# A merged attention and expert kernel, planned with other costs for TensorE's products

## The chip, the cores and the metric

The kernel runs on one core of one Trainium2 chip. The metric is the device time of one execution in microseconds (us). A core has five engines that each take their instructions strictly in the order written: TensorE (PE in the profile, its weight loads as PEld), VectorE (DVE), ScalarE (ACT), GpSimd (POOL) and SyncE (SP, which here only issues DMAs). [...]the order in which the program hands instructions to each engine decides a good part of the time.

## What is computed

The input is x of 8 sequences x 512 tokens x 128 features, float32. Four residual layers follow each other:

```
x = x + attention_a(layernorm(x))   # 16 heads of 8: convolution of 4 taps, silu, delta rule over time
x = x + experts(layernorm(x))       # "f": 8 experts of 256, the best 2 of each token
x = x + attention_b(layernorm(x))   # linear attention in chunks of 128, features elu+1, 16 heads
x = x + experts(layernorm(x))       # "g": the same weights as "f"
```

The delta rule is a recurrence over the 512 tokens of a sequence. For each head with an 8x8 state S:

```
v_new = (v_t - k_t S) * b_t
S     = S + outer(k_t, v_new)
o_t   = q_t S
```

An expert layer computes logits, takes each token's two best experts, and sums relu(x W1[e]) W2[e] with the two normalised weights.

## The kernel before

**Tiling.** Time is cut into 8 chunks (c = 0 to 7) of 64 tokens; a chunk holds 8 sequences x 64 tokens = 512 rows, that is 4 blocks of 128. All 128 pairs of sequence and head lie on the 128 partitions for the recurrence. Each chunk passes through these streams of work:

- `prepare(c)` (L712): layer norm, the convolution as 4 products per q, k, v (`s_pp_a`, L811), silu, norms and the reordering through DRAM.
- `recurring()` (L970): the delta rule, 4 tokens at a time, 16 steps per chunk, 128 in all. A step is four VectorE instructions that depend on each other: `pj`, `factors`, `terms`, `st` (L1003 to L1022). The outputs of a chunk are products on GpSimd (`po`, L1050), summed on VectorE (`o`, L1069).
- `ending(c)` (L1080), then for the chunk `layers` (L1692): output projection (`s_po_a`), experts f (`moe`, L1228), attention b (`linear_attention`, L1661, and `attend`, L1536), experts g. Four lanes hold four chunks at once.
- `moe` sorts the token rows by expert with indirect DMAs on GpSimd, loads the weights of 15 blocks of 128 rows, and does per block two products 128 wide into `s_ph` (L1448), relu on ScalarE into `hT`, and two products into `y_py` (L1460). For the second expert layer of chunk 6, and both expert layers of chunk 7 (which goes in two halves), all experts are computed densely (`all_experts`, L1128), with products 512 or 256 wide.
- `attend` has per block two products `s_pc_b` 512 wide (L1578), whose reader is VectorE's `qs_b`, a `s_pp_b` 384 wide, and products 144 wide (`s_pu_b`, `s_pS_b`).

**What sets the order.** Nothing is ordered by the hardware or by a compiler. While the program is written out, class `Weaver` (L97) plays all streams against each other on an imagined clock per engine. Every instruction goes through `Timed` (L333), which is why nearly all rows of the profile say L343, and `Timed` asks `duration` (L357) what the instruction takes: a pair of time on the engine and of a lag until a reader on another engine may begin. `Weaver.run` (L180) always continues a stream that can begin within `ahead` of the earliest; among those it takes the one with the largest sum of "chain behind it" and a value that `FAVOURED` gives for its part (for instance `("recur", 3)`, the recurrence of chunk 3). The emitted order is then each engine's instruction order.

`tile_hybrid_block_kernel` (L387) first plans without emitting: `PLANS` = 4 rounds, in which the chain behind a step is the longest path of durations from it to the end (`behind`, L216). Then come `PASSES`: 1 round and 35 rounds more in which the chain behind is replaced by the time before the end at which the step begins when the plan is played backwards with busy engines (`before_end`, L224). A last round with `FAVOURED` and `AHEAD_OF` emits the program.

**Filling products.** Before each TensorE instruction, `Weaver.run` hands the planned gap on TensorE to `keep_busy` (L1724). If the gap is at least 0.6 us and a PSUM bank is free, it emits products of a bf16 matrix of ones with itself, 512 wide, whose result nobody reads (`busy`, L1735). Their number follows from the planned gap, and 0.22 us is planned for each:

```
n = int(BUSY * gap / 0.22)        # L1730, BUSY = 0.7
```

**The cost of a TensorE product** in `duration` is, before:

```
if op == "transpose":
    return key, 0.2, 0.15
return key, max(free_size(args[2]) * 1.75e-3, 0.27), 0.15
```

`args[2]` is the moving operand, so `free_size` is the product's width: 128, 144, 256, 384 or 512. A product in the program is one call of `pe.matmul` and is charged once.

Of the kernel before, what the change touches and what calls it, by code (L numbers as in the profile page):

```python
# [19 lines left out]
P = 128  # L20
# [19 lines left out]
PREPARED_ON_POOL = ()  # L40
VALUES_ON_POOL = ()
ADDED_ON_PE = ()
AHEAD_OF = 0
PLANS = 4

LANDS = 3.4
ROWS_LAND = 3.8

PASSES = (
    (1, 0.0, {}),  # L50
    (35, 0.1, {}),
)

FAVOURED = {
    ("b", 0): 365, ("b", 3): 20, ("b", 4): 25, ("b", 5): -8, ("b", 6): -10, ("b", 7): -22, ("b", 7.5): 10,
    ("beside",): -5,
    ("ending",): 4,
    ("f", 0): -43, ("f", 1): 17, ("f", 2): -3, ("f", 3): -3, ("f", 4): -3, ("f", 5): 15, ("f", 6): 309, ("f",
    7): -32, ("f", 7.5): 29,
    ("g", 0): -5, ("g", 3): -13, ("g", 4): -37, ("g", 5): -2, ("g", 6): -15, ("g", 7): 321, ("g", 7.5): 170,  # L60
    ("prepare", 0): -5, ("prepare", 1): -2, ("prepare", 2): -22, ("prepare", 3): 10, ("prepare", 5): -6,
    ("prepare", 7): -10,
    ("recur", 0): 105, ("recur", 1): 98, ("recur", 2): -19, ("recur", 3): -7, ("recur", 4): 10, ("recur", 5):
    -47, ("recur", 6): 15, ("recur", 7): -28,
    ("values",): 14,
}

HALVED = (7,)
# [264 lines left out]
class Timed:  # L333
# [5 lines left out]
    def __getattr__(self, op):  # L339
        call = getattr(self.engine, op)  # L340

        def issue(*args, **kw):
            r = call(*args, **kw)  # L343
            self.weaver.took(*duration(self.key, op, args, kw))
            return r

        return issue


def free_size(ap):  # L350
    n = 1
    for d in ap.shape[1:]:
        n *= d
    return n


def duration(key, op, args, kw):  # L357
    if op == "dma_start":
        return key, 0.4, 0.0, None, LANDS
    if op == "value_load":  # L360
        return key, 0.75, 0.0
    if op == "indirect_dma_start":
        return key, 1.3, 0.0, None, ROWS_LAND
    if key == "PE":
        if op == "transpose":
            return key, 0.2, 0.15
        return key, max(free_size(args[2]) * 1.75e-3, 0.27), 0.15
    out = args[0] if args else kw["out"]
    n = free_size(out)
    if op == "tensor_reduce":  # L370
        n = free_size(args[1])
    if key == "ACT":
        table = TABLE_OF.get(args[2]) if op == "activation" else None
        return key, (0.39 if "bias" in kw else 0.2) + n * 0.76e-3, 0.1, table
    if key == "POOL" and ALU.pow in args:
        return key, 1.05, 0.1
    if key == "POOL":
        return key, 0.15 + n * (1.8e-3 if n > 512 else 2.2e-3), 0.1
    if op == "reciprocal":
        return key, 0.15 + n * 6.5e-3, 0.0  # L380
    if op == "bn_stats":
        return key, 0.28, 0.0
    return key, 0.16 + n * 1.04e-3, 0.0
# [3 lines left out]
def kernel(ctx: ExitStack, tc: tile.TileContext, *tensors: bass.AP):  # L387
# [9 lines left out]
    for n, ahead, favoured in PASSES:  # L397
        for _ in range(n):
# [3 lines left out]
            chains.update(weaver.before_end())  # L402
    merged(ctx, tc, Weaver(chains, FAVOURED, AHEAD_OF), *tensors)

# [1389 lines left out]
```

## Time and profile before

| what | value |
|---|---|
| median of three runs | 951.38 us (951.37 to 951.84) |
| the profiled execution's own time | 1007.78 us |
| its span, first to last instruction | 1006.1 us |
| mean granted TensorE clock | 0.919 |
| instructions | 14877, of these TensorE products 4144 |
| busy: PE, PEld | 834.4 us (83%), 540.9 us (54%) |
| busy: DVE, ACT, POOL | 655.4 us (65%), 523.7 us (52%), 476.3 us (47%) |
| last recurrence step begins (`terms`) | 788.2 us |

The profiled execution takes 1007.78 us where the plain runs take 951.38 us, so a time from the profile stands to a plain one about as 1 to 0.944. The span is 1.7 us shorter than the execution's time.

How to read the rows: a group of instructions names engine, operation and "out<-in" by the program's tiles, then shapes, "x" with their number, busy time and the mean ns of one, then how long the engine had been idle before them and what ended it. Products on PE are pipelined: two in a row overlap, so the sum of busy time is not the sum of their durations, and the distance at which they can follow each other is read from the start times in the timeline. A table by stage gives for each stretch the busy time of each engine with its instruction count, the granted TensorE clock as a fraction of full, the busy share of the DMA engines and GB/s.

### The profile page before, as it was taken

To read this page: it belongs to the slowest core of one execution; us is meant where nothing else is said; L and a number is where in the kernel's file an instruction comes from. 1 tells how busy PE (TensorE), PEld (TensorE's weight loads), DVE (VectorE), ACT (ScalarE), POOL (GpSimd) and SP (SyncE) were. 2 spreads that over 40 slices of the span, in tenths; PEclk is the share of its full clock that TensorE was granted. 3 is DMA by queue.
4 is the path that set the end of the run, shared out by engine and by line. 5 is a ranking of instruction groups with operands and counts; after the bars stand their busy time and mean duration, and the time that the engine had idled before them with its cause. 6 is when DMAs were issued, how large, how long until landed. Compare 5 with 4: busy or idle time off the path is not lost.

```text
span 1006.1 us, 14877 instructions
## 1 busy us (share of the span) xinstructions
PE 834.4 (83%) x4144; PEld 540.9 (54%) x4144; DVE 655.4 (65%) x1625; ACT 523.7 (52%) x1464; POOL 476.3 (47%) x615
## 2 busy tenths in 40 slices
PE   8978697688898887888787788779876848999998
PEld 3332242537453676447643575547745737776566
DVE  1377878648898487788788796688774812264520
ACT  4343255665656456765385475753752526435343
POOL 1133136254646434774367635774366442554530
PEclk9989799799899789899988898989998969999999
DMA  1404504586206464367615574763635636611111
GB/s 27 101 21 116 159 6 127 159 228 189 57 4 178 126 204 129 96 174 222 164 53 161 161 223 126 197 190 102 202 113 155 201 107 169 170 54 48 37 48 38
DMA packets 157989, 126.83 MB, mean 126 GB/s; under 512 B 53105, under 2 KB 123730, under 8 KB 157906
## 3 DMA queue, kind: packets, MB, share of 16 engines
q1 hardware_dynamic: 150674, 112.16, 39.6%
q0 software_dynamic: 6656, 13.64, 4.7%
q8 instruction: 33, 0.54, 0.2%
q14 instruction: 50, 0.41, 0.1%
q10 hardware_dynamic: 576, 0.08, 0.0%
HBM read 91.70 MB, written 36.23 MB: 127 GB/s over the span
## 4 chain that ended last, share of the span: by engine, by line
PE 37%; DVE 28%; ACT 11%; issue 7%; DMA 5%; POOL 5%; another core or an unknown queue 4%; SPq 2%; ACTq 0%; DVEq 0%; POOLq 0%
PE s_ph_g L343 5%; PE y_py_g L343 5%; PE y_py_f L343 4%; PE s_pc_b L343 4%; PE s_pu_b L343 3%; PE s_ph_f L343 3%; DVE st L343 3%; ACT squares L343 3%; DVE factors L343 3%; PE s_pp_a L343 2%; POOL po L343 2%; DVE terms L343 2%; SPq L343 2%; DVE pj L343 2%
## 5 line engine op out<-in xcount | busy, mean ns | idle before, releaser
L1735 PE MATMUL busy<-ones 128*128 128x512 bf16 x514 | 131.5, 403 | 5.3 <-DVE sbd L343 2.4
L343 POOL TENSOR_TENSOR po<-st,kq 128x256 f32<-128x256 f32 x128 | 94.8, 768 | 5.7 <-DVE o L343 5.5
L343 PE MATMUL s_pp_a<-xnT_a,wc 128*128 128x512 f32 x192 | 92.6, 621 | 0.6 <-ACT xnT_a L343 0.6
L343 POOL COPY st<-st 128x64 f32<-128x64 f32 x31 | 8.0, 257 | 175.9 <-DVE st L343 165.5
L1735 PEld LDWEIGHTS <-ones 128*128 128x128 bf16 x514 | 52.1, 104 | 71.3 <-issue 27.2
L343 POOL TENSOR_TENSOR kv_b<-ph_b,v 128x1024 f32<-128x1024 f32 x32 | 63.1, 1974 | 56.8 <-DVE ph_b L343 31.7
L343 PE MATMUL y_py_f<-wt_f,hT_f 128*128 128x128 f32 x420 | 64.7, 308 | 21.5 <-ACT hT_f L343 19.7
L343 ACT ACTIVATE hT_g<-s_ph_g 128x512 f32<-128x512 f32 (+1 forms) x96 | 48.5, 511 | 62.8 <-PE s_ph_g L343 38.2
L343 DVE TENSOR_REDUCE st<-terms 128x64 f32<-128x320 f32 x128 | 62.1, 485 | 24.8 <-ACT terms L343 7.9
L343 ACT COPY terms<-st 128x64 f32<-128x64 f32 x128 | 39.5, 309 | 74.5 <-DVE st L343 64.8
L343 PE MATMUL s_pc_b<-kv_b,tri 128*128 128x512 f32 x128 | 69.7, 648 | 10.3 <-POOL kv_b L343 6.7
L343 PEld LDWEIGHTS y_py_f<-wt_f,hT_f 128*128 128x128 f32 x420 | 58.6, 218 | 28.0 <-ACT hT_f L343 23.6
L343 POOL DMA_INDIRECT there<-m_xw_f,rows_f x56 | 55.9, 999 | 34.2 <-ACT m_xw_f L343 17.6
L343 ACT ACTIVATE hT_f<-s_ph_f 128x512 f32<-128x512 f32 (+1 forms) x88 | 43.7, 501 | 52.8 <-PE s_ph_f L343 38.7
L343 POOL DMA_INDIRECT m_g_f<-back,rows_f x56 | 56.1, 1002 | 31.3 <-issue 15.1
L343 PE MATMUL y_py_g<-wt_g,hT_g 128*128 128x128 f32 x360 | 50.3, 288 | 20.9 <-issue 11.1
L343 DVE TENSOR_REDUCE o<-po 128x64 f32<-128x512 f32 x64 | 42.9, 679 | 34.5 <-POOL po L343 34.5
L343 PE MATMUL s_ph_f<-xsT_f,wt_f 128*128 128x128 f32 x420 | 60.7, 298 | 5.5 <-ACT xsT_f L343 4.5
L343 DVE TENSOR_REDUCE factors<-pj 128x32 f32<-128x288 f32 x128 | 58.8, 460 | 7.4 <-ACT factors L343 3.8
L343 PEld LDWEIGHTS s_ph_f<-xsT_f,wt_f 128*128 128x128 f32 x420 | 56.5, 211 | 10.5 <-ACT xsT_f L343 6.3
L343 PEld LDWEIGHTS s_pp_a<-xnT_a,wc 128*128 128x128 f32 x192 | 36.2, 198 | 43.8 <-issue 37.7
L343 PE MATMUL s_ph_g<-xsT_g,wt_g 128*128 128x128 f32 x360 | 52.2, 296 | 9.0 <-ACT xsT_g L343 3.4
(312 smaller groups left out, 1989.3 us busy)
## 6 DMA issues: line engine op xcount, KB each, us to landing
wt_f<-w SPq DMA_DIRECT2D x105, 256.0 KB
wt_g<-w SPq DMA_DIRECT2D x90, 256.0 KB
scr<-y_a SPq DMA_DIRECT2D x24, 256.0 KB
m_xs_f<-there SPq DMA_DIRECT2D x21, 256.0 KB
back<-yb_f SPq DMA_DIRECT2D x21, 256.0 KB
m_xs_g<-there SPq DMA_DIRECT2D x18, 256.0 KB
back<-yb_g SPq DMA_DIRECT2D x18, 256.0 KB
qk<-scr SPq DMA_DIRECT2D x16, 256.0 KB
```

Source lines behind the costliest of these rows:

```text
L343: r = call(*args, **kw)
L1735: nc.tensor.matmul(pt, ones, ones.unsqueeze(1).to_broadcast([P, 4, P]), start=True, stop=True)
```

## The change

Four settings of the planner change, and nothing else. The streams, tiles, DMAs and arithmetic are the same; the order on each engine and the number of filling products follow anew from the plan.

- A TensorE instruction is planned at 0.9e-3 us per column of its moving operand, at least 0.05 us, widths between 128 and 256 counted as 256, a transpose as 128 wide. Its lag until a reader begins is 0.3 us instead of 0.15 us.
- `PASSES` is empty, so the chains are those of the four rounds of longest paths.
- `AHEAD_OF` is 0.05 us instead of 0.
- `FAVOURED` has other values.

```diff
-AHEAD_OF = 0
+AHEAD_OF = 0.05
...
 PASSES = (
-    (1, 0.0, {}),
-    (35, 0.1, {}),
 )
 
 FAVOURED = {
-    ("b", 0): 365, ("b", 3): 20, ("b", 4): 25, ("b", 5): -8, ("b", 6): -10, ("b", 7): -22, ("b", 7.5): 10,
-    ("beside",): -5,
-    ("ending",): 4,
...
-    ("recur", 0): 105, ("recur", 1): 98, ("recur", 2): -19, ("recur", 3): -7, ("recur", 4): 10, ("recur", 5):
-    -47, ("recur", 6): 15, ("recur", 7): -28,
-    ("values",): 14,
+    ("b", 0): 8, ("b", 1): -301, ("b", 2): -68, ("b", 3): -134, ("b", 4): -200, ("b", 5): -81, ("b", 6): -92,
+    ("b", 7): -216, ("b", 7.5): 390,
+    ("beside",): 215,
+    ("ending",): -74,
...
+    ("outputs",): 217,
...
+    ("recur", 0): -852, ("recur", 1): -89, ("recur", 2): 37, ("recur", 3): -27, ("recur", 4): -282, ("recur",
+    5): -197, ("recur", 6): -116, ("recur", 7): 291,
+    ("values",): 12,
 }
...
     if key == "PE":
-        if op == "transpose":
-            return key, 0.2, 0.15
-        return key, max(free_size(args[2]) * 1.75e-3, 0.27), 0.15
+
+        n = P if op == "transpose" else free_size(args[2])
+        n = 2 * P if P < n < 2 * P else n
+        return key, max(n * 0.9e-3, 0.05), 0.3
```

More of the change, by code (lines that the diff above doesn't have):

```diff
@@ L49 @@
 PASSES = (
-    (1, 0.0, {}),
-    (35, 0.1, {}),
 )
 FAVOURED = {
-    ("b", 0): 365, ("b", 3): 20, ("b", 4): 25, ("b", 5): -8, ("b", 6): -10, ("b", 7): -22, ("b", 7.5): 10,
-    ("beside",): -5,
-    ("ending",): 4,
[L58 to L62, printed above, removed]
-    ("recur", 0): 105, ("recur", 1): 98, ("recur", 2): -19, ("recur", 3): -7, ("recur", 4): 10, ("recur", 5):
-    -47, ("recur", 6): 15, ("recur", 7): -28,
-    ("values",): 14,
+    ("b", 0): 8, ("b", 1): -301, ("b", 2): -68, ("b", 3): -134, ("b", 4): -200, ("b", 5): -81, ("b", 6): -92,
+    ("b", 7): -216, ("b", 7.5): 390,
+    ("beside",): 215,
+    ("ending",): -74,
+    ("f", 0): 2, ("f", 1): 5, ("f", 2): -46, ("f", 3): 79, ("f", 4): 25, ("f", 5): -77, ("f", 6): 105, ("f",
+    7): 30, ("f", 7.5): 245,
+    ("g", 0): 97, ("g", 1): 75, ("g", 2): -94, ("g", 3): 110, ("g", 4): -172, ("g", 5): -398, ("g", 6): -132,
+    ("g", 7): 190, ("g", 7.5): 15,
+    ("outputs",): 217,
+    ("prepare", 0): -61, ("prepare", 1): 150, ("prepare", 2): 32, ("prepare", 3): 24, ("prepare", 4): -223,
+    ("prepare", 5): -10, ("prepare", 6): 38, ("prepare", 7): -418,
+    ("recur", 0): -852, ("recur", 1): -89, ("recur", 2): 37, ("recur", 3): -27, ("recur", 4): -282, ("recur",
+    5): -197, ("recur", 6): -116, ("recur", 7): 291,
+    ("values",): 12,
 }
```

## The prediction

> **What bounds the kernel now.** I read the page's chain first. It belongs to no single engine:
>
> ```profile
> PE 37%; DVE 28%; ACT 11%; issue 7%; DMA 5%; POOL 5%; another core or an unknown queue 4%; SPq 2%; ACTq 0%; DVEq 0%; POOLq 0%
> ```
>
> Then the table by stage, cut where the recurrence ends (790 us) and where TensorE fills up (850 us), and the same table for the filling products alone:
>
> ```profile
> 0.00:200.00 200.00, 158.65 (x624) 72.41 (x624) 127.36 (x309) 88.03 (x258) 55.35 (x132) 0.91 0.33 89
> 200.00:790.00 590.00, 487.09 (x2575) 332.37 (x2575) 454.32 (x1089) 339.81 (x944) 329.49 (x379) 0.91 0.54 152
> 790.00:850.00 60.00, 39.14 (x251) 33.44 (x250) 20.91 (x70) 27.68 (x72) 26.45 (x31) 0.80 0.51 145
> 850.00:1006.00 156.00, 149.56 (x700) 102.64 (x698) 52.77 (x158) 68.22 (x193) 65.00 (x75) 1.00 0.24 67
> ```
>
> ```profile
> 0.00:200.00 200.00, 91.38 (x367) 0.91 0.33 89
> 200.00:790.00 590.00, 35.45 (x132) 0.91 0.54 152
> 790.00:850.00 60.00, 4.09 (x13) 0.80 0.51 145
> 850.00:1006.00 156.00, 0.59 (x2) 1.00 0.24 67
> ```
>
> Columns of the first, after the length: PE, PEld, DVE, ACT, POOL busy, then granted clock. In the middle PE is busy 83% and VectorE 77%: two engines near full that wait for each other. From 850 us on PE is busy 96% at full clock, while VectorE has 53 us to do in 156: that stage ends when PE ends. Fillers are dense only at the start. From 200 us on there are 147 of the 514, so the old plan saw hardly a gap on PE there.
>
> **What a product costs on the chip.** The groups by shape and the timeline of the last stage:
>
> ```profile
> L343 PE MATMUL s_pc_b<-kv_b,tri 128*128 128x512 f32 x128 | 69.7, 648 | 10.3 <-POOL kv_b L343 6.7 <-DVE shift_g L343 3.0 <-DVE ph_b L343 0.2
> ```
>
> ```profile
> 453.01 1.11 PE L343 MATMUL y_py_f<-wt_f,hT_f 128*128 128x128 f32 x8
> 454.06 0.51 PE L343 MATMUL s_pu_b<-v,ph_b 64*128 64x144 f32 x2
> 454.50 0.51 PE L343 MATMUL s_pu_b<-sbd,ident 128*128 128x144 f32 x2
> ```
>
> ```profile
> 934.13 1.02 PE L343 MATMUL s_ph_g<-wt_xsT_g,wc 128*128 128x512 f32 x2
> 934.99 1.02 PE L343 MATMUL s_pc_b<-kv_b,tri 128*128 128x512 f32 x2
> 935.85 1.02 PE L343 MATMUL y_py_g<-hT_g,wc 128*128 128x512 f32 x2
> 936.71 0.81 PE L343 MATMUL s_pp_b<-wb,xn_xnT_b 128*128 128x384 f32 x2
> ```
>
> The program has 8 chunks x 4 blocks x 2 = 64 products `s_pc_b`; the trace has 128. So each float32 product is two instructions on PE. Starts of 512-wide products lie 0.86 us apart (934.99 to 935.85): 0.43 per instruction, 0.86 per product. Four products 128 wide take 1.05 us (453.01 to 454.06), so about 0.25 each; one 144 wide takes 0.44. (Transposes are one instruction, 0.11 apart in the rows of the same timeline.) Against that:
>
> - 512 wide: 0.86 on the chip, planned 0.896 before, 0.461 after.
> - 128 wide: 0.25, planned 0.27 before, 0.115 after.
> - 144 wide: 0.44, planned 0.27 before, 0.23 after.
> - transpose: 0.11, planned 0.2 before, 0.115 after.
>
> The new cost is the distance between two instructions in a row, charged once per product: right for transposes, half the truth for the products.
>
> Here a rule speaks for the change. The Trainium skill, Perfetto Trace Analysis, section Engine Utilization, gives the array 307.2 G output elements a second, halved for FP32_LOW_HIGH. Read as the price of a whole product, 128x512 elements at 153.6 G/s are 0.43 us, and the new 0.461 is right. Then the fillers below would find real gaps and the sum would be no more than the clock's gain. The rows say 0.43 per instruction with two instructions per product, and I follow the rows.
>
> **The change, part by part.** *Planned PE time.* From the instruction counts by shape, two per float32 product: 231 products 512 wide, 138 of 256, 33 of 384, 876 of 128, 188 of 144, 97 narrower than 10, 439 transposes, 65 small bf16 ones. Before, in that order: 207 + 62 + 22 + 237 + 51 + 26 + 88 + 18 = 711 us planned. After: 106 + 32 + 11 + 101 + 43 + 5 + 51 + 3 = 352 us. On the chip at full clock, with 0.1 per narrow instruction and 0.06 per bf16 one: 199 + 59 + 21 + 219 + 83 + 19 + 48 + 4 = 652 us. The old plan is 9% above the chip, the new one 46% below.
>
> *Filling products.* Their number is worked out from planned gaps. I take 951 us for the old plan's length, an estimate: gaps 951 - 711 = 240 us, of which 514 x 0.22 = 113 us, or 47%, were filled. After, a plan of the same length has 951 - 352 = 599 us of gaps; the same share is 281 us, some 1,280 fillers. If the plan shrinks to 800 us, gaps are 448, filled 210 us, 955 fillers. So 440 to 765 are added; I take 600. On the chip 26 of them start over 5.7 us at full clock (31.87 to 37.59 in the timeline), 0.22 each, so 132 us are added to an engine already busy 83% of the span. Shared out like PE's busy time without fillers (67, 452, 35 and 149 us by stage): 13, 85, 7 and 28 us.
>
> *What hides them.* PE is idle 41, 103, 21 and 6 us in the four stages. But a filler stands in PE's queue ahead of a real product, and the plan's gaps aren't the chip's, since real products take twice as long as planned. I let half of the idle time absorb fillers where it is long: 20, 51, 10, and all 6 in the last.
>
> *The clock.* With more fillers PE stays warm. The clock is granted at 0.91 in the first two stages, 0.80 in the third: bringing all to 1.00 would save 14, 44 and 8 us of PE's busy time. The Trainium skill, TensorE: Matmul & The Clock Gate, section HAM oscillation, says that idle gaps beyond about 3.4 us throttle the array; by it, full warmth is worth those 66 us on PE. The row limits it: the last stage already has 1.00 with 2 fillers, so it gains nothing, and PE is 37% of the chain. I take two thirds of it, 9, 29 and 5 us.
>
> First stage 13 - 20 - 9, at best nothing to pay; second 85 - 51 - 29 = 5; third 7 - 10 - 5, nothing; last 28 - 6 = 22. I count no gain from the surplus, since no chain of PE's alone runs through it. Together **+27 us**. Bounds: 440 fillers with all idle time absorbing give no loss and the clock's gain, 25 us (37% of 66); 765 fillers with a quarter absorbed cost about 85.
>
> *Readers.* VectorE reads each 512-wide `s_pc_b`. A pair takes 1.02 us from start to end; planned until the reader begins are 0.461 + 0.3 = 0.761 after (1.046 before). The reader `qs_b` is put into VectorE's queue 0.26 us early, and behind it in order stand the recurrence's four instructions, `o`, and the routing's small ones: 64 x 0.26 = **+17 us** on an engine busy 77%. Rows of 8 products, 2 us on the chip and 0.9 planned, do the same to ScalarE's `hT`, which has 48% free; nothing there, with 20 us if `terms` is what stands behind. Bounds of readers: 0 (covered by idle time) to 35.
>
> *Order by `FAVOURED`, no `PASSES`, `AHEAD_OF`.* No instruction is added, but all move, in every queue: SP's weight loads and row stores, GpSimd's indirect DMAs and `po`, ScalarE's table switches. No row prices that. The nearest bounds: VectorE is idle 136 us in the middle, and the recurrence needs 1.79 us (418 + 460 + 423 + 485 ns) x 128 = 229 us of the 738 it spans, so a better order could end it earlier by tens of us; a worse one costs as much. One further wait like VectorE's `o` on `po` (20 us in the middle) is the nearest size. I take 0, ends -25 and +25.
>
> Sum: 1007.78 + 27 + 17 = 1052 us for a profiled execution; times 951.38 / 1007.78 = 0.944: **993 us**.
>
> **The rivals.** A, the sum, 0.62. B: fillers sink into idle time, the order is somewhat worse, with one more wait of 20 us: 1028 x 0.944 = 970 us, 0.17. For it: PE idles 171 us. Against: its idle in the last stage is 6. C, the other side: warmth. If the fillers fit and hold the clock at 1.00, 25 us come off the chain; with an order that ends the recurrence some 20 us earlier, 963 x 0.944 = 909; clock alone 928. It decides if added fillers cost less than 66 us of PE plus the idle time they fall in, chiefly if few go into the last stage. For it: the plan still knows VectorE's times, and PE's cheapness puts VectorE's chain first. Against: all the products' ends are planned too early. 928 us, 0.16. D, the plan comes out nearly alike: 951 us, 0.05; against it, half of PE's planned time is gone.
>
> **How the numbers follow.** Measurement tells apart about 0.2%, 2 us. Faster 0.16, same 0.05, slower 0.79. Range 935 to 1045: the low end takes in B and C's half nearer to no change; the high end is 1007.78 + 85 + 35 less 20 for idle time that both would use, 1108, times 0.944. Outside lie half of C, 0.08, and the worse end of A with a worse order, about 0.1.
>
> **What would show it.** Fillers between 950 and 1,300, most after 200 us; clock above 0.96; PE busy over 90% in the middle; PE's last stage longer than 156 us or with dozens of fillers. Wrong if fillers stay near 514 (the sum's main term falls), if the clock rises and PE's busy time doesn't, or if the last recurrence step begins well before 788 us.

## The result, and the profile after

The changed kernel takes 1008.95 us (median of three runs, 1005.69 to 1010.35) where the kernel before takes 951.38. The ratio is 1.060, with a 95% interval of 1.056 to 1.064: 58 us slower. Forecast were 993 us and slower.

The first profile of before, on which the prediction was built, turned out to be of an execution of 1007.78 us, 6% longer than its timed runs. A second profile of the same kernel has an execution of 953.93 us, and it is the one to hold against the profile after (1005.69 us). The chain of waits of the changed kernel, and below it that of the second profile of before:

```profile
PE 63%; DVE 20%; issue 6%; ACT 5%; POOL 4%; DMA 1%; SPq 0%; DVEq 0%; ACTq 0%; POOLq 0%
```

```profile
PE 34%; DVE 32%; ACT 11%; POOL 7%; issue 6%; DMA 6%; SPq 2%; DVEq 0%; ACTq 0%; POOLq 0%
```

TensorE's share of the chain nearly doubled, VectorE's fell from 32% to 20%. The stages now (a stage is a stretch of the execution), cut at 200 us and where the last recurrence step ends (columns as in the prediction's first table: length, PE, PEld, DVE, ACT, POOL busy, granted clock, DMA share, GB/s), first the changed kernel, then the second profile of before:

```profile
0.00:200.00 200.00, 172.18 (x699) 82.69 (x700) 117.10 (x280) 88.42 (x247) 52.93 (x127) 0.91 0.35 94
200.00:774.00 574.00, 529.31 (x2869) 340.41 (x2868) 426.53 (x1049) 325.90 (x900) 314.07 (x369) 0.95 0.53 150
774.00:1004.00 230.00, 220.99 (x1165) 156.25 (x1164) 102.96 (x298) 113.95 (x317) 109.02 (x119) 1.00 0.33 96
```

```profile
0.00:200.00 200.00, 159.84 (x634) 74.22 (x635) 128.58 (x311) 89.75 (x262) 57.21 (x134) 0.91 0.34 91
200.00:750.00 550.00, 475.48 (x2564) 325.45 (x2563) 453.29 (x1088) 339.13 (x938) 327.75 (x376) 0.93 0.56 162
750.00:952.20 202.20, 184.93 (x950) 132.55 (x948) 73.86 (x228) 95.69 (x265) 92.87 (x106) 0.99 0.34 96
```

The middle is 24 us longer and the stage after the recurrence 28 us. In the middle PE is busy 92% instead of 86%, VectorE 74% instead of 82%. The fillers went from 514 to 1,099; their group in the profile after, and what of it lies in the last stage (the changed kernel, then the second profile of before):

```profile
L1737 PE MATMUL busy<-ones 128*128 128x512 bf16 x1099 | 268.8, 392 | 6.6 <-DVE ph_b L344 3.2
```

```profile
774.00:1004.00 230.00, 17.27 (x68) 1.00 0.33 96
```

```profile
750.00:952.20 202.20, 4.21 (x15) 0.99 0.34 96
```

The last stage is longer because the new order leaves more for it: without fillers 1,097 TensorE instructions instead of 935, and 298 of VectorE instead of 228, with TensorE busy 96% of it.

The largest waits of VectorE for a TensorE product, in total us, number and longest wait; the changed kernel first, then the second profile of before:

```profile
DVE sbd L344 <- PE s_pu_b L344: 34.8, 26, 5.3
DVE qs_b L344 <- PE s_pc_b L344: 27.1, 31, 3.4
DVE x_a L344 <- PE s_po_b L344: 19.5, 7, 7.0
DVE dn_b L344 <- PE s_pS_b L344: 18.3, 13, 3.6
DVE x_a L344 <- PE s_pty_g L344: 14.8, 2, 10.0
DVE up_f L344 <- PE y_pl_f L344: 10.6, 5, 7.3
```

```profile
DVE x_a L343 <- PE s_pty_g L343: 37.6, 3, 17.2
DVE qs_b L343 <- PE s_pc_b L343: 20.8, 20, 6.8
DVE sbd L343 <- PE s_pu_b L343: 17.0, 21, 2.9
DVE dn_b L343 <- PE s_pS_b L343: 10.3, 8, 3.9
DVE x_a L343 <- PE s_po_a L343: 10.0, 5, 7.1
DVE qs_b L343 <- PE s_pk_b L343: 9.4, 6, 3.2
DVE x_a L343 <- PE s_po_b L343: 3.0, 3, 1.8
```

Not every one of these waits grew. Summed over all such rows, stage by stage:

| VectorE waits for TensorE, us | before, second profile | changed kernel |
|---|---|---|
| to 200 us | 4.1 | 10.1 |
| the middle | 29.7 | 60.4 |
| after the recurrence | 81.6 | 63.8 |
| the whole span | 115.5 | 134.2 |

The middle is where they count. There VectorE's busy time fell by 27 us (453.3 to 426.5) and its waits for all engines rose by 51 (69.9 to 121.2), of which 31 for TensorE; the difference is the 24 us by which the middle grew.

The longest of the 26 waits at `sbd` (their mean is 1.3 us), seen from both queues of the changed kernel. VectorE first, then TensorE over the same stretch (start, us, instruction, number):

```profile
647.99 0.30 DVE L344 TENSOR_TENSOR sbd<-s_pu_b,hmask 128x144 f32<-128x144 f32 x1
648.20 0.41 DVE L344 TENSOR_TENSOR ph_b<-s_pp_b,mn_b 128x256 f32<-128x256 f32 x1
653.93 0.31 DVE L344 TENSOR_TENSOR sbd<-s_pu_b,hmask 128x144 f32<-128x144 f32 x1 [5.32 <-PE s_pu_b L344]
...
656.66 0.41 DVE L344 TENSOR_TENSOR pj<-st,factors 128x256 f32<-128x256 f32 x1
```

```profile
644.64 2.77 PE L344 MATMUL s_ph_g<-xsT_g,wt_g 128*128 128x128 f32 x12
647.20 2.87 PE L344 MATMUL y_py_g<-wt_g,hT_g 128*128 128x128 f32 x16
650.00 1.03 PE L344 MATMUL s_pn_a<-sq,hmask 128*16 128x512 f32 x2
650.96 2.05 PE L344 MATMUL s_ph_g<-xsT_g,wt_g 128*128 128x128 f32 x16
652.95 0.51 PE L344 MATMUL s_pu_b<-v,ph_b 64*128 64x144 f32 x2
```

The table by stage over two parts of that stretch (the clock is the third number from the end):

```profile
644.00:649.00 5.00, 5.00 (x25) 5.00 (x25) 4.41 (x10) 3.06 (x7) 3.29 (x5) 0.50 0.17 46
650.00:653.00 3.00, 3.00 (x20) 2.03 (x19) 0.00 (x0) 1.35 (x3) 3.00 (x4) 1.00 0.74 186
```

VectorE stands still for 5.32 us at `sbd`, and the next recurrence step, `pj`, starts only at 656.66 behind it. TensorE is not idle and runs no filler: it works off 6 + 8 + 1 + 8 real products ahead of `s_pu_b`. The new cost plans these at 0.69 + 0.92 + 0.46 + 0.92 = 3.0 us; from 644.64 to 652.95 they took 8.3. At full clock, by the distances that the prediction read off, they would take about 6.4 (an estimate: 22 x 0.25 + 0.86); the rest goes with the granted clock of 0.50 up to 649 us. So the price is not all of this wait, but the larger part of the 5.3 us that were lost against the plan.

The planner's own clock can be laid beside the trace, since VectorE's 1,611 planned instructions stand in the trace in the order in which they were emitted, alike in kind one by one. Before this `sbd` it has VectorE idle for 0.40 us. Before all 56 `sbd` that read `s_pu_b` it plans 4.4 us of idle time, where the chip waits 34.8 (kernel before: 5.6 planned, 17.0 on the chip); before `qs_b` 4.9, where the chip waits 30.9 for `s_pc_b` and `s_pk_b` (before: 28.7 planned, 30.2 on the chip). At `qs_b` the old plan foresaw the waits, the new one did not.

### The profile page after: what moved, and what is told of

Its sections match the earlier page's. It is cut to its first block, busy times and chain, and to the rows that moved or that the text cites. A ratio compares the mean times of both kernels' runs of the same rounds, so it can differ in the third digit from the quotient of the medians.

```text
span 1004.0 us, 16075 instructions
## 1 busy us (share of the span) xinstructions
PE 922.5 (92%) x4729; PEld 579.4 (58%) x4729; DVE 646.6 (64%) x1625; ACT 528.3 (53%) x1463; POOL 476.0 (47%) x615
## 4 chain that ended last, share of the span: by engine, by line
PE 63%; DVE 20%; issue 6%; ACT 5%; POOL 4%; DMA 1%; SPq 0%; DVEq 0%; ACTq 0%; POOLq 0%
PE s_pp_a L344 8%; PE busy L1737 7%; PE s_ph_g L344 7%; PE y_py_g L344 6%; PE s_ph_f L344 6%; PE y_py_f L344 6%; PE s_pc_b L344 5%; PE s_pu_b L344 4%; DVE spare L344 3%; PE s_pS_b L344 2%; DVE W L344 2%; POOL po L344 2%; DVE st L344 2%; PE s_pt_f L344 2%; ACT squares L344 1%
## 5 line engine op out<-in xcount | busy, mean ns | idle before, releaser
L1737 PE MATMUL busy<-ones 128*128 128x512 bf16 x1099 | 268.8, 392 | 6.6 <-DVE ph_b L344 3.2
L1737 PEld LDWEIGHTS <-ones 128*128 128x128 bf16 x1099 | 109.5, 102 | 134.6 <-issue 34.8
L344 POOL TENSOR_TENSOR po<-st,kq 128x256 f32<-128x256 f32 x128 | 90.8, 738 | 4.4 <-DVE o L344 4.0
L344 PE MATMUL s_pp_a<-xnT_a,wc 128*128 128x512 f32 x192 | 85.9, 596 | 0.0
L344 POOL DMA_INDIRECT there<-m_xw_f,rows_f x56 | 58.9, 1051 | 19.8 <-issue 9.4
L344 POOL DMA_INDIRECT there<-m_xw_g,rows_g x48 | 47.5, 989 | 31.2 <-ACT m_xw_g L344 14.7
L344 DVE TENSOR_TENSOR qs_b<-s_pc_b,ph_b 128x512 f32<-128x512 f32 x64 | 43.1, 686 | 27.1 <-PE s_pc_b L344 27.1
L344 DVE TENSOR_TENSOR pj<-st,factors 128x256 f32<-128x256 f32 x128 | 53.5, 418 | 11.0 <-ACT factors L344 7.9
L344 PE MATMUL s_ph_f<-xsT_f,wt_f 128*128 128x128 f32 x420 | 55.8, 284 | 2.5 <-ACT xsT_f L344 2.4
L344 PEld LDWEIGHTS s_ph_f<-xsT_f,wt_f 128*128 128x128 f32 x420 | 52.6, 199 | 8.4 <-ACT xsT_f L344 3.8
```

The costliest lines, as they stand in the source:

```text
L1737: nc.tensor.matmul(pt, ones, ones.unsqueeze(1).to_broadcast([P, 4, P]), start=True, stop=True)
```

## Experiments

Two theories came out of the prediction. *Fillers*: the 585 added fillers crowd TensorE. *Order*: they sit in idle time, and the new sequence costs. The second one split up later into *price* (products planned at half their cost) and *fit* (favoured values are good for the one plan that they were chosen with). Beside the chip's times I read, for each kernel, where the planner's own imagined clock ends for the emitted round, an output of the program and no measurement of the chip: 904 us before, 821.5 after.

**before_again: the kernel before, unchanged.**

> The kernel before, unchanged, profiled once more: its profiled execution took 1007.78 us where its plain runs took 951.38. If that execution was an odd one, this profile shows a span near 950 us and the same 514 fillers, and it is the one to compare with; if profiling stretches this kernel by 6%, the span is near 1006 us again. Ratio 1.00 in either case.

Measured 946.44 us, ratio 0.998 (0.995 to 1.001); profiled execution 953.93 us, 514 fillers, clock 0.940. The first profile was the odd one; profiling does not stretch this kernel.

**after_thin and after_none: the changed plan with fewer fillers.** In `keep_busy` the plan's clock is left alone; only the emission is thinned, r = 514/1099, and 0:

```diff
-            pt = ps.tile([P, 4, P], F32, tag=f"s{i}", name="busy")
-            for _ in range(n):
+            emitted[1] += n
+            m = int(emitted[1] * r) - emitted[0]
+            emitted[0] += m
+            if m > 0:
+                pt = ps.tile([P, 4, P], F32, tag=f"s{i}", name="busy")
+            for _ in range(m):
```

> The changed plan with the same order on every engine and the same planned clocks, but with 514 of its 1,099 filling products emitted, spread evenly. Theory of the fillers: 585 x 0.214 = 125 us leave TensorE, and most of the 57 us lost come back: 955 to 975 us. Theory of the order (the fillers sit in idle time, and what costs is the new sequence): 1000 to 1012 us.

Measured 1006.12 us, ratio 1.063 (1.060 to 1.067): nothing came back. TensorE's busy time fell from 922 to 824 us and the clock from 0.954 to 0.910, the span went from 1004.0 to 1001.3. The fillers' own busy time fell by 126 us, that of the other products rose by 27 at the lower clock. So this is a net result: a cost of the fillers as large as what their warmth gives back is not excluded by it.

> The changed plan with its order but with no filling product at all. Theory of the fillers: 940 to 975 us, at a granted clock below 0.90, the lost warmth giving back part of what the free queue gains. Theory of the order: above 1000 us, and more with a colder clock.

Measured 1021.69 us, ratio 1.079 (1.075 to 1.083), clock 0.832. Without any filler it is slower. The theory of the fillers, which had 940 to 975 us, falls for this change: no number of them that was tried makes the new order fast. Net of what they may cost, the warmth that they give is worth about 2%.

**before_more: the plan of before with 1,099 fillers** (the same edit on the kernel before, r = 1099/514).

> The plan of before with its order, but with 1,099 filling products emitted instead of 514, each at the places where the plan of before puts some. Theory of the fillers: 975 to 1005 us, though two thirds of them fall in the first 200 us, where TensorE has idle time, which could keep it at 965. Theory of the order: 951 to 960 us.

Measured 998.79 us, ratio 1.054 (1.050 to 1.058), as the theory of the fillers had it. More fillers do cost where they overfill the places that a plan had for them: each planned gap now holds 2.14 x 0.7 = 1.5 times its length, and in the first 200 us PE is busy 197 us. The first recurrence step begins at 70 us instead of 51, the last at 798 instead of 749.

**before_nudge: a meaningless change of the cost.**

```diff
-        return key, max(free_size(args[2]) * 1.75e-3, 0.27), 0.15
+        return key, max(free_size(args[2]) * 1.76e-3, 0.27), 0.15
```

> The kernel before with one meaningless change: a TensorE product is planned at 1.76e-3 us per column instead of 1.75e-3, 0.6% more; the lag, the passes and the favoured values stay. Theory of the price (the plan is bad because the products' cost is wrong): nothing real changes, 940 to 960 us. Theory of the fit (the favoured values fit the one plan that they were chosen for, and any other cost throws it off): 975 to 1010 us, about what the change itself lost.

Measured 983.85 us, ratio 1.038 (1.029 to 1.047). The planner's clock ends at 968 us instead of 904. A cost moved by 0.6% costs more than half of what the whole change cost: the fit exists.

**before_newcost: the new cost and lag alone, in the kernel before.** The diff is the last hunk of the change.

> The kernel before with the new TensorE cost and lag alone; passes, favoured values and the window stay. Theory of the price: about the changed kernel's 1009 us or worse, 995 to 1030. Theory of the fit: also slow, 975 to 1020, so this run tells them apart only together with the other three.

Measured 1104.62 us, ratio 1.162 (1.152 to 1.172), worse than either theory gave. The planner's clock ends at 912 us, nearly as for before; the chip ends 192 us later.

**after_oldcost and after_pair: the changed kernel with other costs.** The first puts the old hunk back; the second charges a float32 product twice:

```diff
-        return key, max(n * 0.9e-3, 0.05), 0.3
+        pair = op != "transpose" and not (n % NE == 0 and n <= (HB + 1) * NE)
+        return key, max(n * 0.9e-3, 0.05) * (2 if pair else 1), 0.3
```

> The changed kernel with the old TensorE cost and lag put back; its favoured values, empty passes and window stay. Theory of the price: the plan is right again for the products, 955 to 985 us, clearly under 1009. Theory of the fit: its favoured values were chosen for the new cost, so it gets worse or stays: 1000 to 1050 us.

> The changed kernel, with the new cost charged twice for a float32 product (two instructions on TensorE) and once for transposes and bf16 products: 0.92 us planned for 512 columns where the trace shows 0.86, 0.23 for 128 where it shows 0.25. Everything else as changed. Theory of the price: 950 to 980 us, the best of these four. Theory of the fit: 1000 to 1060 us, since no favoured value was chosen for this cost.

Measured 1045.36 us (1.100, 1.092 to 1.109) and 1109.18 us (1.166, 1.157 to 1.176). The first lies where the fit had it, the second 49 us above even that range, and both far above what the price had. The favoured values of the change don't carry over to another cost, not even to one close to the trace. But the planner's clock ends at 1012 and 1071 us, and the chip is only 33 and 38 us behind. That is what the price does: in the four combinations of old and new cost with the old and the new other settings, it sets how far the chip is behind the plan. It is not that a shorter plan is harder to meet: before_newcost and the kernel before have nearly the same plan.

| kernel | planner's end | chip | chip behind plan |
|---|---|---|---|
| before | 904 | 951 | 47 |
| before_nudge | 968 | 984 | 16 |
| after_oldcost | 1012 | 1045 | 33 |
| after_pair | 1071 | 1109 | 38 |
| changed kernel | 821.5 | 1009 | 188 |
| before_newcost | 912 | 1105 | 192 |

The next three and the last run were on another chip, where the kernel before takes 1002 to 1003 us; their ratios are to that. The changed kernel itself was not run there, and only the kernel before was run on both chips, so that a ratio carries over from one to the other is assumed here and not shown.

**after_plain and before_plain: no favoured values.** `FAVOURED = {}` in either kernel.

> The changed kernel with FAVOURED empty. The planner's own clock ends at 906 us for it, at 821 for the changed kernel. So far the chip ended 188 and 192 us after the planner's clock where products are planned at the new cost, and 16 to 47 us after it where they are planned at the old one or at twice the new one. Theory of the price and the fit together (the new cost makes every plan about 190 us too short, and the favoured values win back on the chip what they win in the plan): 1080 to 1115 us. Theory that the favoured values chosen under the new cost are worth nothing on the chip: 1000 to 1030 us.

> The kernel before with FAVOURED empty. The planner's clock ends at 940 us instead of 904. Price and fit together: 956 to 990 us. If the favoured values of before are worth nothing on the chip: 945 to 955 us. Against the run before this one it shows what the costs, the passes and the window make of an order that nobody tuned.

Measured 1140.49 us, ratio 1.137 (1.131 to 1.143), and 1018.57 us, ratio 1.018 (1.013 to 1.023). At 951 us for the kernel before these would be 1081 and 968, within what price and fit gave. The chip is 234 us behind the plan in the first, 78 in the second, and 98 for the kernel before on this chip: the price again. If the ratios carry over, values chosen under the wrong cost are worth something on the chip too: 85 us in the plan (906 to 821), and 7% of the kernel before (1.137 to 1.060). And values that no longer fit can be worse than none: before_nudge has 1.038, before_plain 1.018 (968 against 940 us in the plan).

**fit_after: a cost as the trace shows it, with favoured values searched for it.**

```diff
-        n = 2 * P if P < n < 2 * P else n
-        return key, max(n * 0.9e-3, 0.05), 0.3
+        if op == "transpose" or n % NE == 0 and n <= (HB + 1) * NE:
+            return key, max(n * 0.9e-3, 0.06), 0.2
+        return key, 0.44 if P < n < 2 * P else max(n * 1.69e-3, 0.25 if n == P else 0.2), 0.2
```

> The changed kernel (no passes, window 0.05) with a TensorE cost as the trace shows it: a float32 product 1.69e-3 us per column (0.865 at 512), 0.25 at 128, 0.44 at 144, at least 0.2; transposes 0.115; lag 0.2; and with favoured values searched anew on the planner's clock, 9,000 tries from those of the change (1050 to 914 us). Price and fit together: 914 plus 16 to 47, so 930 to 961 us, 50 us or more under the changed kernel. Theory that it is only the missing passes that cost: 990 us or more.

Measured 1032.27 us, ratio 1.029 (1.025 to 1.033), which at 951 would be 979 us: between the expectation of 930 to 961 and that of the other theory, 990 or more. It wins back about half of the loss and doesn't beat the kernel before. The planner's clock ended at 914 us, 10 above that of before; the chip was 118 us behind it where the kernel before, on this chip, is 98 behind its own. The rest of the miss isn't explained; that the missing passes cost something is a rival which no run tests alone.

**after_upper: the changed plan on products that cost no more than it planned.** Each float32 product reads the upper halves of its operands as bf16 (products in bf16's precision, transposes left alone):

```diff
+def upper(ap):
+    at = (slice(None),) * (len(ap.shape) - 1)
+    return ap.bitcast(BF16)[at + (slice(1, None, 2),)]
...
-            r = call(*args, **kw)
+            given = args
+            if op == "matmul" and not isinstance(args[1], Shape) and args[1].dtype == F32:
+                given = (args[0], upper(args[1]), upper(args[2]))
+            r = call(*given, **kw)
```

> The changed kernel with its plan untouched, its order, fillers and DMAs as they are, but each float32 product reads only the upper halves of its operands as bf16. So a product is one instruction on TensorE, planned at 0.461 us for 512 columns and by the fillers' 0.214 not dearer than that. It changes the arithmetic: the products have bf16's precision; transposes stay float32. The planner's clock ends at 821 us. Theory of the price (the order is a good one, for products at half their true cost): the chip ends 16 to 47 us after the planner's clock as it does where the cost is right, 837 to 870 us on a chip where the kernel before takes 950, 885 to 920 where it takes 1002. Theory that the new order is poor in itself (favoured values, no passes, window): 950 us or more.

Measured 876.34 us, ratio 0.873 (0.868 to 0.879), 55 us behind the planner's clock, and 9 us under the range expected for this chip. (A fourth execution took 1596 us, of which the cause is not known; it is left out.) The order is the changed one, its 1,099 fillers are all there, and now it is fast. But the products are even cheaper than planned: in the rows below two of 512 columns and eight of 128 each have 0.92 us in the plan.

```profile
508.46 0.61 PE L347 MATMUL s_pc_b<-kv_b,tri 128*128 128x512 bf16 x2
514.01 0.62 PE L347 MATMUL s_ph_f<-xsT_f,wt_f 128*128 128x128 bf16 x8
```

Its chain, and VectorE's waits for the same products as above:

```profile
DVE 45%; PE 14%; issue 13%; POOL 10%; ACT 9%; DMA 4%; another core or an unknown queue 3%; SPq 1%; DVEq 0%; POOLq 0%; ACTq 0%
```

```profile
DVE dn_b L347 <- PE s_pS_b L347: 6.9, 4, 5.3
DVE x_a L347 <- PE s_pty_g L347: 6.7, 2, 3.8
DVE sbd L347 <- PE s_pu_b L347: 6.5, 4, 4.2
DVE x_a L347 <- PE s_po_b L347: 4.8, 1, 4.8
DVE qs_b L347 <- PE s_pc_b L347: 4.1, 5, 1.4
```

34.8 us of waits at `sbd` became 6.5, 27.1 at `qs_b` became 4.1, and all of VectorE's waits for TensorE went from 134.2 to 42.1. So the new order is fast where its products take no longer than it was planned for. But any order may gain from a TensorE this fast: the same edit on the kernel before was not run, so this says nothing on how the two orders compare with cheap products.

## Why the prediction was right, and where it wasn't

The sign and the cause at its root were right: a cost that is half the truth for the products. The size came near, 58 us lost and 42 forecast, by luck: the largest term of the sum measured nil, and what it left out made up for it.

- *The cost.* "Right for transposes, half the truth for the products": right, and it decides how far the chip falls behind its plan: 47 and 33 us with the old cost, 188 and 192 with the new. The rule of the Trainium skill (Perfetto Trace Analysis, Engine Utilization), read as pricing a whole product at 0.43 us, was rightly set aside for the rows. Planned PE time of 711 and 352 us came out as worked out: the planner's own sums, less 0.22 us for each filler, are 710 and 352.
- *The number of fillers.* 1,099, within 955 to 1,280.
- *What the fillers cost*, the main term of the sum, +27 us: wrong. Taking 585 of them away changed nothing (1.063 against 1.060), cost and warmth taken together. The step that failed is "I let half of the idle time absorb fillers", together with what was allowed for the clock: idle time and the clock's gain paid for all of them, in which shares isn't shown. It hangs on where they stand: the same number put into the old plan cost 5.4%.
- *The clock.* 0.954, not above 0.96, and the kernel before has 0.940 in its second profile, not 0.919: little was left to win. That no filler at all costs 2%, at a clock of 0.832, fits the rule that the prediction cites (the Trainium skill, TensorE: Matmul & The Clock Gate, HAM oscillation), that idle gaps throttle the array.
- *Readers*, +17 us: the right place and too small. VectorE's waits for TensorE in the middle rose by 31 us, from 29.7 to 60.4, close to the upper bound of 35; over the whole span they rose by only 19, because those of the last expert layers fell. I priced a reader by its own product (0.26 us early). A reader is early by all that stands ahead of its product in TensorE's queue: 1.3 us in the mean of 26 waits at `sbd`, 5.32 at most.
- *Order*, taken as 0: failed as a step of its own. It shows in the last stage, 28 us longer with 162 more TensorE instructions left for it. The price and the order can't be told apart by adding them. In the planner's clock the new settings won 82.5 us (904 to 821.5); on the chip the plan was 188 us short instead of 47, which lost 141. The difference is 58 us, the whole result.
- *The base.* The sum stood on a profile of an odd execution. In it the last recurrence step begins at 788 us; in the second profile at 749, and after the change at 774. Against the first profile the recurrence seemed to end earlier by 14 us, against the right one it ends 24 us later. The size hardly suffered: unscaled, the terms are 44 us instead of 42. Rival C's argument, that VectorE's chain would come first, failed with that.

Of the rivals, B's wording ("fillers sink into idle time, the order is somewhat worse") describes what happened better than A's, at A's size.

What stays open: which of the three settings (`PASSES`, `AHEAD_OF`, `FAVOURED`) does what on the chip was not run. In the plan none wins the 82.5 us alone: with any one of them put back in the changed kernel, the planner's clock ends at 895, 891 and 904 us in that order, so they fit only each other. Open is also why fit_after was 20 us further behind its plan than the kernel before.

## What to carry to other kernels

Before a planner's cost is changed, count instructions per call in the trace and measure starts of calls, not of instructions: here every float32 product is two. A plan's own end is worth nothing until one knows how far the chip is behind it; compare that gap first, then the plans. And values tuned to a plan belong to it: a cost moved by 0.6% cost 3.8%, so a change of cost can be judged only after tuning anew.

## What the runs showed of the hardware

- Chips differ for this kernel: 951 and 948 us in some sets of runs, 1002 in others. All four traces from the other chip have stretches put down to "another core or an unknown queue" in the chain that ended last: 15 us in after_plain, 39 in before_plain, 28 in fit_after and in after_upper. The first profile of before has 45; its time and its clock of 0.919 lie among those of the kernel before on the other chip (996 to 1008 us, 0.918 to 0.929), so it may come from there; on which chip it ran isn't recorded. The second profile of before has none, nor has any other trace. What holds the engines there wasn't found.
- In the changed order 1,099 products of bf16 ones on TensorE, 269 us of busy time at a granted clock of 0.954, make no measurable difference to 514 at 0.910, and none at 0.832 costs about 2%: in this kernel warmth is a small matter against order.
